# Attention, layer norm and five gated graph steps on one core: Strassen's block sums moved from accumulating DMA to VectorE

## The chip, the cores and the metric

The kernel runs on one core of a Trainium2 chip. The metric is the device time of one execution in microseconds (us). Lower is better.

A core has five engines that work side by side, each with its own queue of instructions, and waits for one another by semaphores: TensorE (PE in the profile: matrix products, its weight loads are PEld), VectorE (DVE), ScalarE (ACT), GpSimd (POOL) and SyncE (SP), which here only issues transfers (DMA). Products land in PSUM; everything else on the chip lies in SBUF.

## The reference

The input x has 16 images of 1024 rows by 128 columns, and one adjacency matrix `adj` (1024 x 1024, entries 0 or 1) serves all of them. Two layers follow each other, each with a residual and a layer norm without weights:

```python
# layer 0: graph attention
h = x @ others_weight
e = u1[:, idx1] + u2[:, idx2]            # u1 = h @ a1, u2 = h @ a2
att = softmax(where(adj > 0, leaky_relu(e), NEG_BIG), axis=1)
x = layernorm(x + att @ h + x @ self_weight)

# layer 1: five steps of a gated graph network, adj in both directions
for _ in range(5):
    m = adj @ h                           # m_in and m_out are the same here
    av = concat([m, m])
    u3 = h @ w_u3.T + b_u3
    z = sigmoid(av @ w3.T + b3 + u3)
    r = sigmoid(av @ w4.T + b4 + u3)
    hv = tanh(av @ w5.T + b5 + (r * h) @ w_u5.T + b_u5)
    h = (1 - z) * h + z * hv
out = layernorm(x + h)
```

## The kernel before

**The work of a step.** Images go in pairs q = 0 to 7 (images `one` = 2q and `two` = 2q + 1), and a pair goes through five steps s. A step has three parts. `messages(q, s, k)` makes m = adj h for both images, `gates(b, s, soon)` makes z, r, hv and the new h of one image, and `leave(b, s)` sends the new h on to the next step. The state h is kept transposed, `hT` (128 features by 1024 rows), in two halves of 128 x 512.

**High and low parts.** [...]`split` writes a block of h as two parts: ScalarE casts it to fp32r (L571), and VectorE subtracts the cast from the original for the rest (L575). A product then has two terms per chunk, and `product` (L583) issues eight matmuls for a block of 512 rows.

**Strassen.** The product of adj, as 2 x 2 quarters of 512 x 512, with the two images, whose halves form the other 2 x 2 matrix, is done in Winograd's form of Strassen's method: seven block products in place of eight. It needs sums of quarters of adj (made once, `tab`) and in each step four sums of blocks of h: s1, s2, s3 and s4. With X11, X12 the halves of `one` and X21, X22 those of `two`, the kernel overwrites in turn X22 += X21 (s1), X21 += X11, X11 += X22 (s2; X21 is s3) and X12 += X11 (s4). The signs that this needs are carried by the images themselves: even images are stored negated (`sign`). 34 of the 40 pair steps go this way; six, named in `PLAIN`, use eight plain products (`L1010`).

**How a block comes to `messages`.** `leave` turns 32 x 32 blocks of hT on VectorE (`turn`, L529), and four transfers put them in their places in a buffer X in device memory (`away`, L539); `back` (L547) loads X into a tile F. The sums are made there too: `add_to` (L559) is a transfer issued by GpSimd that adds one X to another in device memory. So a Strassen step loads seven times: x12, x11 and x22 as they are (F_x_x in the profile), and s1 to s4 after the sums (F_x_s). X buffers are [128, 512] blocks of 256 KB, and the loads and sums of one step are tied in order by the entries `("turn", "F", k)` and `("turn", "blk", k)`.

**Gates.** Each half of an image has one product u3 h into PSUM (L1099), which ScalarE copies to a second bank (gz, L1102) so that r and z can both be added to it (L1109), then tanh on ScalarE (L1112), r h on VectorE (L1119), two products for hv (L1125, L1126), tanh (L1129), and three VectorE operations to the new hT (L1136, L1143, L1150).

**Layer 0** is `layer0(b)`: the attention's products, a normalisation (`layernorm`: statistics on VectorE, the power on GpSimd, the scaling on ScalarE), and the way to the first step. `on_pe(b, what)` says where a transpose is made on TensorE instead of by VectorE and transfers: for the first two images and for the last step of the last three.

**The order.** All instructions are put down in a plan first. Each has an engine, an assumed length, a rank and the values it reads and writes; `Plan.order` then runs a small simulation. Whenever an engine is free, the ready instruction of the lowest rank is taken whose tiles are to be had. The lengths of VectorE's and ScalarE's work are taken `MARGIN` (1.2) times, and `LAG` stands for the time from one engine to another. Each engine then carries out its instructions strictly in the order that comes out. Ranks come from `rank_of` (10 per pair, 4.5 per step), `rank0` for layer 0, and small offsets `D` for each kind. So work of two or three pairs is in flight together. `IDLE` puts in transposes of the identity with the rank 9000, which are taken only where the plan sees TensorE without other work; they keep its clock up.

**Buffers.** `kinds` gives the number of tiles of each sort: `blk` 8 (split blocks), `F` 4 (loads of X, and those of layer 0 and of the output), `m` 5 (messages), `part` 1 and `yT` 2 (layer 0), `T` 3, `hT` 6, and in PSUM six banks `ps` and two `gz`.

Of the kernel before, what the change touches and what calls it, by code (L numbers as in the profile page):

```python
# [9 lines left out]
F32 = mybir.dt.float32  # L10
# [3 lines left out]
ALU = mybir.AluOpType  # L14
AX = mybir.AxisListType

P = 128
N = 1024
HALF = 512
NC = N // P  # L20
STEPS = 5
# [4 lines left out]
LOW, HIGH = -20.0, 100.0  # L26
TINY = 1e-30
PLAIN = {(0, 0), (0, 1), (0, 2), (7, 2), (7, 3), (7, 4)}
IDLE = 24


class Plan:
# [4 lines left out]

    MARGIN = 1.2  # L40
    SAME = {"PE": 0, "DVE": 60, "ACT": 60, "POOL": 60, "SP": 2500, "DMA": 0}
    LAG = {"PE": 250, "DVE": 150, "ACT": 170, "POOL": 200, "SP": 2500, "DMA": 2400}

# [87 lines left out]
def kernel(  # L131
# [51 lines left out]
    nc = tc.nc  # L183
    B = x_t.shape[0]
# [6 lines left out]
    wsi = const.tile([P, P], F32, tag="wsi", name="wsi")  # L191
# [8 lines left out]
    ident = const.tile([P, P], F32, tag="ident", name="ident")  # L200
# [10 lines left out]
    def exact(pools):  # L211

        def pool(name, bufs, space=None):
# [11 lines left out]
            "pb": (1, [P, N], F32, None),  # L225
            "blk": (8, [P, 2, NC // 2, P], F32R, None),
            "yT": (2, [P, HALF], F32, None),
            "part": (1, [P, HALF], F32, None),
            "junk": (1, [P, HALF], F32, None),
            "y0": (2, [P, NC // 2, P], F32, None),  # L230
            "hT": (6, [P, N], F32, None),
            "T": (3, [P, HALF], F32, None),
            "F": (4, [P, HALF], F32, None),
            "m": (5, [P, HALF], F32, None),
            "r": (3, [P, HALF], F32, None),
            "z": (3, [P, HALF], F32, None),
            "hv": (2, [P, HALF], F32, None),
# [21 lines left out]
        def T(t, dtype=None, shape=None):  # L259
            if t not in tiles:  # L260
                _, sh, dt, _ = kinds[t[0]]
                tiles[t] = places[t[0]].tile(
                    shape or sh, dtype or dt, tag=t[0], name="_".join(map(str, t)).replace("-", "n")
                )
            return tiles[t]
# [12 lines left out]
        plan = Plan({tag: k[0] for tag, k in kinds.items()})  # L278
# [3 lines left out]
        def pe(*a, **k):  # L282
            plan.add("PE", *a, **k)

        def dve(*a, **k):
            plan.add("DVE", *a, **k)

        def act(*a, **k):
            plan.add("ACT", *a, **k)

        def sp(*a, **k):
            plan.add("SP", *a, **k)


        D = dict(m=-0.4, pu=0.8, u=0, pr=0.0, pz=0.2, r=-0.3, pv=0.0, z=0.5, hv=0.4, h=0.6, tr=1.0, o=3.4, ln=3.5)
        D.update(out=4.2, l1=-7, l2=-6, l3=-6, l4=-4, l5=-3, l6=-2.5, l7=-1, l8=0)

        def on_pe(b, what):

            return b < 2 and what in ("y", "b") or b >= B - 3 and what == STEPS - 1  # L300

        def plain(q, s):

            return (q, s) in PLAIN

        def rank_of(b, s):
            return 10 * (b // 2) + 4.5 * s

        def rank0(b):
            return 10 * (b // 2) + -2.5  # L310

        def sign(b):

# [93 lines left out]


        def idle_():
            for j in range(4):  # L410
                nc.tensor.transpose(T(("ps", "idle"))[:, j * P : (j + 1) * P], ident, ident)


# [4 lines left out]
            pe(F, -99, lambda k=k: fill_(k), reads=[(("ident",), 0)], writes=[(("gz", "fill", k), 0)])  # L418

        for i in range(IDLE):  # L420
            pe(4 * TR, 9000, idle_, reads=[(("ident",), 0)], writes=[(("ps", "idle"), 0)])

        def self_():
            nc.vector.tensor_tensor(wsi, W("ws"), ident, ALU.add)
# [91 lines left out]
        def transposes(src, read, t, rank):  # L516


            def emit():
                for j in range(4):  # L520
                    nc.tensor.transpose(T(t)[:, j * P : (j + 1) * P], src()[:, j * P : (j + 1) * P], ident)

            pe(4 * TR, rank, emit, reads=[*read, (("ident",), 0)], writes=[(t, 0)])
# [19 lines left out]
        def back(d, t, rank, also=(), then=()):  # L543
            sp(
                450,
                rank,
                lambda: nc.sync.dma_start(T(t), T(d)[:, 0:HALF]),  # L547
                reads=[(d, 0), *also],
                writes=[(t, 0), *then],
                lag=2300,  # L550
            )

        def add_to(d, other, rank):

            plan.add(
                "POOL",
                1000,
                rank,
                lambda: nc.gpsimd.dma_start(T(d)[:, 0:HALF], T(other)[:, 0:HALF], accum_op=ALU.add),  # L559
                reads=[(other, 0), (d, 0)],  # L560
                writes=[(d, 0)],
                lag=3500,
            )

        def split(blk, src, read, rank, then=()):
# [27 lines left out]
        def layer0(b):  # L593

            first = rank0(b) - (60 if b == 0 else 0)
            rank = first + D["l1"]
# [240 lines left out]
            right = slice(HALF, N)  # L837
            for g in range(2):
                po = ("ps", "acc", b, "po", g)
                part = (yT[0], "p") if g == 0 else (("part", b), "p")  # L840

                def part_(g=g, po=po, part=part):
                    nc.vector.tensor_tensor(T(part[0]), T(po), pairs()[:, g, :], ALU.mult)

                for c0 in range(0, 4, size):
                    cs = range(c0, c0 + size)

                    def po_(g=g, po=po, cs=cs):
                        product(po, hl[0][g], quarter(g, 0), cs[0] == 0, cs[-1] == 3, cs)

                    pe(
                        2 * size * R,
                        rank,
                        po_,
                        reads=[(k, 4 * g + c, j) for k, j in ((hl[0][g], 0), (hl[0][g], 1), (("A",), 0)) for c in cs],
                        writes=[(po, 0)],
                    )
                dve(V, rank, part_, reads=[(po, 0), (pb, 0), (pb, 1)], writes=[part])

            def add_():  # L860
                nc.vector.tensor_tensor(T(yT[0]), T(yT[0]), T(("part", b)), ALU.add)

            dve(V, rank, add_, reads=[(yT[0], "p"), (("part", b), "p")], writes=[(yT[0], "s")])
            px = ("ps", "acc", b, "px")
            pe(
                F,
                rank,
                lambda: nc.tensor.matmul(T(px), wsi, T(xt)[:, left], start=True, stop=True),
                reads=[(xt, 0), (("wsi",), 0), (("part", b), "p")],
                writes=[(px, 0)],  # L870
            )
            dve(
# [13 lines left out]
            for g in range(2):  # L886
# [4 lines left out]
                    reads=[(k, 4 * g + c, j) for k, j in ((hl[1][g], 0), (hl[1][g], 1), (("A",), 1)) for c in range(4)],  # L891
                    writes=[(po2, 0)],
                )
            act(A, rank, lambda: nc.scalar.copy(T(yT[1]), T(po2)), reads=[(po2, 0)], writes=[(yT[1], 0)])

            for g in range(2):
                rank = rank0(b) + D["l5"]
# [77 lines left out]
        def messages(q, s, k):  # L975
# [5 lines left out]
            def by_chunk(t):  # L981
                return T(t).rearrange("p (c a j) -> p c a j", c=4, a=4) if s == 0 else chunks(T(t))

            def from_dram(b, g, blk, last=False):
                t = ("F", "x", *blk[1:])
                entered = [(("hT", x), "in") for x in (one, two)] if s == 0 else []
                back(
                    ("X", b, s, g), t, rank, [(("turn",), "F", k - 1), *entered], [(("turn",), "F", k)] if last else ()
                )
                split(  # L990
                    blk,
                    lambda: by_chunk(t),
                    [(t, 0), (("turn",), "blk", k - 1)],
                    rank,
                    [(("turn",), "blk", k)] if last else (),
                )

            def multiply(bank, blk, right, of, first, last, onto=()):
# [10 lines left out]

            if plain(q, s):  # L1010
                for b in (one, two):
                    blks = [("blk", b, "h", s, g) for g in range(2)]
                    if s:
                        for g in range(2):
                            from_dram(b, g, blks[g], b == two and g == 1)
                    for e in range(2):
                        bank, m = ("ps", "acc", b, s, e), ("m", b, s, e)
                        for g in range(2):
                            multiply(bank, blks[g], quarter(g, e), y(g, e), g == 0, g == 1)
                        act(  # L1020
                            A,
                            rank + D["m"],
                            lambda bank=bank, m=m: nc.scalar.copy(T(m), T(bank)),
                            reads=[(bank, 0)],
                            writes=[(m, 0)],
                        )
                return [[(("m", b, s, e), 0) for e in range(2)] for b in (one, two)]

            def X(b, g):
                return ("X", b, s, g)  # L1030

            blk = {k: ("blk", q, s, k) for k in ("x11", "x12", "x22", "s1", "s2", "s3", "s4")}
            t = [(("tab",), c, k) for c in range(4) for k in range(2)]
            from_dram(one, 1, blk["x12"])
            from_dram(one, 0, blk["x11"])
            from_dram(two, 1, blk["x22"])
            add_to(X(two, 1), X(two, 0), rank)
            from_dram(two, 1, blk["s1"])
            add_to(X(two, 0), X(one, 0), rank)
            add_to(X(one, 0), X(two, 1), rank)  # L1040
            from_dram(one, 0, blk["s2"])
            from_dram(two, 0, blk["s3"])
            add_to(X(one, 1), X(one, 0), rank)
            from_dram(one, 1, blk["s4"], True)

            a, b, c = (("ps", "acc", q, s, "a"), ("gz", q, s), ("ps", "acc", q, s, "c"))
            m = {(x, e): ("m", x, s, e) for x in (one, two) for e in range(2)}
# [107 lines left out]
        def leave(b, s):  # L1155
# [3 lines left out]
            for g in range(2):  # L1159
# [2 lines left out]
                    return T(hT)[:, g * HALF : (g + 1) * HALF]  # L1162

                k, d = ("T", b, s, g), ("X", b, s + 1, g)
                if s < STEPS - 1:
                    turn(k, h, [(hT, g)], rank + D["tr"])
                    away(k, d, rank + D["tr"])
                    continue
# [376 lines left out]
```

## Time and profile before

| | |
|---|---|
| median of 3 runs | 1603.84 us |
| lowest and highest | 1602.44 and 1603.89 us |
| span of the profiled execution | 1594.5 us |
| mean granted TensorE clock | 0.968 |
| VectorE busy | 1094.1 us |
| ScalarE busy | 891.5 us |
| L559, 136 accumulating transfers | 4.8 us to land (median) |
| L571, casts of summed blocks | 136 of 619 ns |
| L575, subtractions for them | 136 of 684 ns |
| L1136, a VectorE sum of two SBUF tiles | 684 ns |
| L411, idle transposes | 96, from 4 to 23 us |

A line of the profile's groups or waits begins with the line of the kernel and the engine, and then gives the tiles as out<-in. A wait "A <- B: t, n, longest" says that engine A stood still in front of A's instruction for t us in n cases, until B was done. A row of the table of stretches gives the length, busy time and count for PE, PEld, DVE, ACT and POOL, then the granted clock, the share of the DMA engines and the GB/s.

### The profile page before, as it was taken

Reading aid. Unit: us, or ns where it says so; the run is one execution under the profiler, and the core shown is the slowest. Engines: PE = TensorE matmul, PEld = TensorE weight load, DVE = VectorE, ACT = ScalarE, POOL = GpSimd, SP = SyncE. Lnnn points to the kernel's source line nnn. Section 1 sums busy time; section 2 is a strip of 40 time slices with the busy share of each in tenths; the row PEclk is TensorE's granted clock in tenths of the full one; section 3 lists DMA queues with packets and bytes.
Section 4 is the critical chain, followed back from the end, with each engine's and each line's share of the span. In section 5 each row is a group of like instructions: output and inputs, shape, how many; then the busy total and the mean of one; then the engine's idle time right before and its main releaser. Section 6 shows DMA issues by size and latency. Waiting matters only on the chain. (4 is left out here: it accounts for less than half of the span.)

```text
span 1594.5 us, 18201 instructions
## 1 busy us (share of the span) xinstructions
PE 1478.0 (93%) x4932; PEld 908.5 (57%) x4932; DVE 1094.1 (69%) x2625; ACT 891.5 (56%) x1792; POOL 260.1 (16%) x401
## 2 busy tenths in 40 slices
PE   8998899899998999999889989998899999999994
PEld 6665566565555556655565555665566555555552
DVE  6877678677865768668676677766678566665434
ACT  4546556565555655566555556565556555544434
POOL 0202003012120121212221121111302022101002
PEclk9999999999999999999999999999999999999997
DMA  4145666766686667776566665766667666553221
GB/s 164 60 120 158 173 157 181 185 152 161 152 225 154 145 152 169 198 166 155 142 167 189 155 158 141 185 180 157 153 154 178 169 164 139 125 127 93 78 66 42
DMA packets 245540, 238.74 MB, mean 150 GB/s; under 512 B 39007, under 2 KB 164662, under 8 KB 245430
## 3 DMA queue, kind: packets, MB, share of 16 engines
q1 hardware_dynamic: 225282, 200.99, 43.2%
q0 software_dynamic: 19584, 35.66, 15.9%
q10 hardware_dynamic: 564, 0.85, 0.2%
q8 instruction: 40, 0.66, 0.2%
q14 instruction: 70, 0.57, 0.1%
HBM read 158.07 MB, written 114.99 MB: 171 GB/s over the span
## 5 line engine op out<-in xcount | busy, mean ns | idle before, releaser
L559 POOL DMA_DIRECT2D X<-X x136 | 114.3, 840 | 891.2 <-DMA X<-X 310.5
L571 ACT CAST blk_s<-F_x_s 128x512 fp32r<-128x512 f32 x136 | 83.6, 619 | 201.9 <-DMA F_x_s<-X 198.2
L1109 PE MATMUL ps_g_r<-m,wm 128*128 128x512 f32 x320 | 162.6, 607 | 23.8 <-ACT gz L1102 22.1
L1126 PE MATMUL ps_g_v<-r,u5h 128*128 128x512 f32 x320 | 166.6, 602 | 12.5 <-DVE r L1119 12.5
L583 PE MATMUL ps_acc_a<-tab,blk_s 128*128 128x512 f32 x544 | 156.9, 430 | 17.6 <-ACT m L1052 13.3
L1125 PE MATMUL ps_g_v<-m,wm 128*128 128x512 f32 x320 | 164.3, 595 | 0.0
L1109 PE MATMUL gz<-m,wm 128*128 128x512 f32 x320 | 161.1, 604 | 0.0
L1136 DVE TENSOR_TENSOR hv<-hv,hT 128x512 f32<-128x512 f32 x160 | 109.3, 684 | 72.6 <-ACT hv L1129 72.1
L1099 PE MATMUL ps_g_r<-hT,u 128*128 128x512 f32 x320 | 154.4, 595 | 0.0
L575 DVE TENSOR_TENSOR blk_s<-F_x_s,blk_s 128x512 fp32r<-128x512 f32 x136 | 92.6, 684 | 83.8 <-ACT blk_s L571 83.5
L1119 DVE SCALAR_TENSOR_TENSOR r<-r,hT 128x512 f32<-128x512 f32 x160 | 109.3, 687 | 54.4 <-ACT r L1112 53.7
L583 PE MATMUL ps_acc_po<-adj,blk 128*128 128x512 f32 x512 | 145.5, 429 | 0.0
L583 PEld LDWEIGHTS ps_acc_a<-tab,blk_s 128*128 128x128 f32 x544 | 105.4, 198 | 62.4 <-ACT m L1052 22.3
L1112 ACT ACTIVATE r<-ps_g_r,bh 128x512 f32<-128x512 f32 x160 | 108.9, 685 | 37.3 <-PE ps_g_r L1109 37.0
L583 PEld LDWEIGHTS ps_acc_po<-adj,blk 128*128 128x128 f32 x512 | 96.1, 188 | 40.3 <-issue 17.3
L583 PE MATMUL ps_acc<-adj,blk_h 128*128 128x512 f32 x384 | 104.3, 431 | 14.2 <-ACT blk_h L571 8.6
L1112 ACT ACTIVATE z<-gz,bh 128x512 f32<-128x512 f32 x160 | 109.4, 687 | 9.6 <-PE gz L1109 9.2
L1126 PEld LDWEIGHTS ps_g_v<-r,u5h 128*128 128x128 f32 x320 | 59.9, 191 | 94.4 <-issue 57.4
L529 DVE STREAM_TRANSPOSE T<-hT 128x512 f32<-128x512 f32 x154 | 108.5, 705 | 5.7 <-DMA X<-T 3.6
L1109 PEld LDWEIGHTS ps_g_r<-m,wm 128*128 128x128 f32 x320 | 59.9, 193 | 90.7 <-issue 45.6
L1143 DVE SCALAR_TENSOR_TENSOR hv<-z,hv 128x512 f32<-128x512 f32 x160 | 108.6, 680 | 3.0 <-ACT z L1112 1.8
L1150 DVE SCALAR_TENSOR_TENSOR hT<-hv,hT 128x512 f32<-128x512 f32 x160 | 108.4, 679 | 1.8
(165 smaller groups left out, 2445.5 us busy)
## 6 DMA issues: line engine op xcount, KB each, us to landing
X<-T SPq DMA_DIRECT2D x616, 64.0 KB
X<-X POOLq DMA_DIRECT2D x136, 256.0 KB, 4.8
F_x_s<-X SPq DMA_DIRECT2D x136, 256.0 KB
F_x_x<-X SPq DMA_DIRECT2D x102, 256.0 KB
yd<-y SPq DMA_DIRECT2D x32, 256.0 KB
o<-yd SPq DMA_DIRECT2D x32, 256.0 KB
out_dram<-o SPq DMA_DIRECT2D x32, 256.0 KB
xt<-in_x_dram SPq DMA_DIRECT2D x15, 512.0 KB
```

Of the source, the lines that this page charges most:

```text
L529: nc.vector.transpose(T(t).rearrange("p (b c i) -> p b c i", b=4, c=4), turned(src()))
L559: lambda: nc.gpsimd.dma_start(T(d)[:, 0:HALF], T(other)[:, 0:HALF], accum_op=ALU.add),
L583: nc.tensor.matmul(T(bank), T(blk)[:, k, c, :], right(c), start=(first and i == 0), stop=(last and i == len(terms) - 1), skip_group_check= ...
L1099: nc.tensor.matmul(T(pr), u3, h(), start=True, stop=True)
L1109: nc.tensor.matmul(T(p_), wm[:, j, :], T(m), start=False, stop=True, skip_group_check=True)
L1112: nc.scalar.activation(T(t), T(p_), AF.Tanh, bias=bh[:, j : j + 1], scale=0.5 * sg)
L1119: lambda r=r, h=h: nc.vector.scalar_tensor_tensor(T(r), T(r), 1.0, h(), ALU.add, ALU.mult),
L1125: nc.tensor.matmul(T(pv), wm[:, 2, :], T(m), start=True, stop=False)
L1126: nc.tensor.matmul(T(pv), u5h, T(r), start=False, stop=True)
L1136: lambda hv=hv, h=h: nc.vector.tensor_tensor(T(hv), T(hv), h(), ALU.subtract),
L1143: lambda hv=hv, z=z: nc.vector.scalar_tensor_tensor(T(hv), T(z), 1.0, T(hv), ALU.add, ALU.mult),
L1150: lambda hv=hv, h=h: nc.vector.scalar_tensor_tensor(h(), T(hv), 0.5, h(), ALU.mult, ALU.add),
```

## The change

Five things change.

1. The block sums are made on VectorE. The four halves f11, f12, f21, f22 of a pair are loaded once each into tiles of a new sort G (4), in the order f11, f12, f21, f22. `halves` splits x11, x12 and x22 from them, and `add_to` becomes a VectorE addition inside those tiles. The transfers that accumulate, and three loads of each Strassen step, are gone.
2. Tiles for G come from others: F has 2 instead of 4, m has 4 instead of 5, and `part` is gone. In layer 0 the second partial product goes to yT[1] instead, and the copy into yT[1] waits for the sum that reads it.
3. The last pair is staggered: the plain steps of image 15 get a rank higher by `LATER` = 3, and step 3 of the last pair is transposed on TensorE (`TURNED`), so that its blocks are split directly from PSUM.
4. Ranks and offsets are set anew, and `MARGIN` is 1.15.
5. There are 100 idle pieces of two transposes instead of 24 of four.

```diff
-IDLE = 24
+LATER = 3
+TURNED = {(7, 3)}
+IDLE = 100
...
-    MARGIN = 1.2
+    MARGIN = 1.15
...
-            "part": (1, [P, HALF], F32, None),
...
-            "F": (4, [P, HALF], F32, None),
-            "m": (5, [P, HALF], F32, None),
+            "G": (4, [P, HALF], F32, None),
+            "F": (2, [P, HALF], F32, None),
+            "m": (4, [P, HALF], F32, None),
...
-        D = dict(m=-0.4, pu=0.8, u=0, pr=0.0, pz=0.2, r=-0.3, pv=0.0, z=0.5, hv=0.4, h=0.6, tr=1.0, o=3.4, ln=3.5)
-        D.update(out=4.2, l1=-7, l2=-6, l3=-6, l4=-4, l5=-3, l6=-2.5, l7=-1, l8=0)
+        D = dict(m=-0.4, pu=1.4, u=0.4, pr=0.8, pz=1.4, r=-0.3, pv=0.2, z=0.3, hv=0.2, h=0.6, tr=1.0, o=3.6, ln=3.9)
+        D.update(out=4.2, l1=-9, l2=-5, l3=-4, l4=-4, l5=-5, l6=-3.5, l7=-1, l8=0)
...
-            return b < 2 and what in ("y", "b") or b >= B - 3 and what == STEPS - 1
+            return b < 2 and what in ("y", "b") or b >= B - 3 and what == STEPS - 1 or (b // 2, what) in TURNED
...
-            return 10 * (b // 2) + 4.5 * s
+            return 10 * (b // 2) + 4.2 * s + (LATER if b == B - 1 and plain(b // 2, s) else 0)
...
-            return 10 * (b // 2) + -2.5
+            return 10 * (b // 2) - 1 * (1 - b % 2) + -1.0
...
-            for j in range(4):
+            for j in range(2):
                 nc.tensor.transpose(T(("ps", "idle"))[:, j * P : (j + 1) * P], ident, ident)
...
-        def add_to(d, other, rank):
-
-            plan.add(
-                "POOL",
-                1000,
-                rank,
-                lambda: nc.gpsimd.dma_start(T(d)[:, 0:HALF], T(other)[:, 0:HALF], accum_op=ALU.add),
-                reads=[(other, 0), (d, 0)],
-                writes=[(d, 0)],
-                lag=3500,
-            )
...
-                part = (yT[0], "p") if g == 0 else (("part", b), "p")
+                part = (yT[g], "p")
...
+            def from_dram(b, g, i):
+                t, x = ("G", b, s, g), ("X", b, s, g)
+                turn = [(("turn",), k, i - 1) if i else (("turn",), k - 1, 3)]
                 entered = [(("hT", x), "in") for x in (one, two)] if s == 0 else []
+                sp(0, rank, lambda: T(t), reads=[(x, 0), *turn, *entered], writes=[(t, "place"), (("turn",), k, i)], lag=0)
+                back(x, t, rank, [(t, "place")])
+                return t
...
+            def add_to(t, other):
+                dve(
+                    V,
+                    rank,
+                    lambda: nc.vector.tensor_tensor(T(t), T(t), T(other), ALU.add),
+                    reads=[(other, 0), (t, 0)],
+                    writes=[(t, 0)],
+                )
...
-            from_dram(one, 1, blk["x12"])
-            from_dram(one, 0, blk["x11"])
-            from_dram(two, 1, blk["x22"])
-            add_to(X(two, 1), X(two, 0), rank)
-            from_dram(two, 1, blk["s1"])
-            add_to(X(two, 0), X(one, 0), rank)
-            add_to(X(one, 0), X(two, 1), rank)
-            from_dram(one, 0, blk["s2"])
-            from_dram(two, 0, blk["s3"])
-            add_to(X(one, 1), X(one, 0), rank)
-            from_dram(one, 1, blk["s4"], True)
+            f11, f12, f21, f22 = (from_dram(x, g, 2 * (x == two) + g) for x in (one, two) for g in range(2))
+            halves(blk["x11"], f11)
+            halves(blk["x12"], f12)
+            halves(blk["x22"], f22)
+            add_to(f22, f21)
+            halves(blk["s1"], f22)
+            add_to(f21, f11)
+            add_to(f11, f22)
+            halves(blk["s2"], f11)
+            halves(blk["s3"], f21)
+            add_to(f12, f11)
+            halves(blk["s4"], f12, True)
...
+                if s < STEPS - 1 and on_pe(b, s):
+                    t = ("ps", "t", b, s, g)
+                    transposes(h, [(hT, g)], t, rank + D["tr"])
+                    split(
+                        ("blk", b, "h", s + 1, g),
+                        lambda t=t: T(t).rearrange("p (c a j) -> p c a j", c=4, a=4),
+                        [(t, 0)],
+                        rank_of(b, s + 1),
+                    )
+                    continue
```

More of the change, by code (lines that the diff above doesn't have):

```diff
@@ L420, in exact @@
         for i in range(IDLE):
-            pe(4 * TR, 9000, idle_, reads=[(("ident",), 0)], writes=[(("ps", "idle"), 0)])
+            pe(2 * TR, 9000, idle_, reads=[(("ident",), 0)], writes=[(("ps", "idle"), 0)])
         def self_():
@@ L860, in add_ @@
             def add_():
-                nc.vector.tensor_tensor(T(yT[0]), T(yT[0]), T(("part", b)), ALU.add)
-            dve(V, rank, add_, reads=[(yT[0], "p"), (("part", b), "p")], writes=[(yT[0], "s")])
+                nc.vector.tensor_tensor(T(yT[0]), T(yT[0]), T(yT[1]), ALU.add)
+            dve(V, rank, add_, reads=[(yT[0], "p"), (yT[1], "p")], writes=[(yT[0], "s")])
             px = ("ps", "acc", b, "px")
@@ L868, in layer0 @@
                 lambda: nc.tensor.matmul(T(px), wsi, T(xt)[:, left], start=True, stop=True),
-                reads=[(xt, 0), (("wsi",), 0), (("part", b), "p")],
+                reads=[(xt, 0), (("wsi",), 0), (yT[1], "p")],
                 writes=[(px, 0)],
@@ L893, in layer0 @@
                 )
-            act(A, rank, lambda: nc.scalar.copy(T(yT[1]), T(po2)), reads=[(po2, 0)], writes=[(yT[1], 0)])
+            act(A, rank, lambda: nc.scalar.copy(T(yT[1]), T(po2)), reads=[(po2, 0), (yT[0], "s")], writes=[(yT[1], 0)])
             for g in range(2):
@@ L982, in by_chunk, with halves @@
                 return T(t).rearrange("p (c a j) -> p c a j", c=4, a=4) if s == 0 else chunks(T(t))
-            def from_dram(b, g, blk, last=False):
-                t = ("F", "x", *blk[1:])
+            def from_dram(b, g, i):
+                t, x = ("G", b, s, g), ("X", b, s, g)
+                turn = [(("turn",), k, i - 1) if i else (("turn",), k - 1, 3)]
                 entered = [(("hT", x), "in") for x in (one, two)] if s == 0 else []
-                back(
-                    ("X", b, s, g), t, rank, [(("turn",), "F", k - 1), *entered], [(("turn",), "F", k)] if last else ()
-                )
+                sp(0, rank, lambda: T(t), reads=[(x, 0), *turn, *entered], writes=[(t, "place"), (("turn",), k, i)], lag=0)
+                back(x, t, rank, [(t, "place")])
+                return t
+            others = []
+            def halves(blk, t, last=False):
                 split(
@@ L992, in from_dram @@
                     lambda: by_chunk(t),
-                    [(t, 0), (("turn",), "blk", k - 1)],
+                    [(t, 0), (("turn",), "blk", k - 1), *(((x, 0) for x in others) if last else ())],
                     rank,
                     [(("turn",), "blk", k)] if last else (),
+                )
+                others.append(blk)
+            def add_to(t, other):
[5 more added lines that the diff above has]
+                    writes=[(t, 0)],
                 )
@@ L1011, in messages @@
                 for b in (one, two):
+                    rank = rank_of(b, s)
                     blks = [("blk", b, "h", s, g) for g in range(2)]
-                    if s:
+                    if s and not on_pe(b, s - 1):
                         for g in range(2):
-                            from_dram(b, g, blks[g], b == two and g == 1)
+                            halves(blks[g], from_dram(b, g, 2 * (b == two) + g), b == two and g == 1)
                     for e in range(2):
@@ L1027, in messages @@
                 return [[(("m", b, s, e), 0) for e in range(2)] for b in (one, two)]
-            def X(b, g):
-                return ("X", b, s, g)
             blk = {k: ("blk", q, s, k) for k in ("x11", "x12", "x22", "s1", "s2", "s3", "s4")}
             t = [(("tab",), c, k) for c in range(4) for k in range(2)]
-            from_dram(one, 1, blk["x12"])
-            from_dram(one, 0, blk["x11"])
-            from_dram(two, 1, blk["x22"])
-            add_to(X(two, 1), X(two, 0), rank)
-            from_dram(two, 1, blk["s1"])
-            add_to(X(two, 0), X(one, 0), rank)
-            add_to(X(one, 0), X(two, 1), rank)
-            from_dram(one, 0, blk["s2"])
-            from_dram(two, 0, blk["s3"])
-            add_to(X(one, 1), X(one, 0), rank)
-            from_dram(one, 1, blk["s4"], True)
+            f11, f12, f21, f22 = (from_dram(x, g, 2 * (x == two) + g) for x in (one, two) for g in range(2))
[10 more added lines that the diff above has]
+            halves(blk["s4"], f12, True)
             a, b, c = (("ps", "acc", q, s, "a"), ("gz", q, s), ("ps", "acc", q, s, "c"))
```

## The prediction

> **What bounds the kernel now.** I read the page first, then the waits of all engines, those of SyncE's DMA queue, the timeline of one long stall, and last a table of stretches.
>
> From the page: busy shares, the slices, the queues.
>
> ```profile
> PE 1478.0 (93%) x4932; PEld 908.5 (57%) x4932; DVE 1094.1 (69%) x2625; ACT 891.5 (56%) x1792; POOL 260.1 (16%) x401
> ...
> PEclk9999999999999999999999999999999999999997
> ...
> q1 hardware_dynamic: 225282, 200.99, 43.2%
> q0 software_dynamic: 19584, 35.66, 15.9%
> ```
>
> TensorE is the bound: its matmuls leave little free. A busy matmul row is not a full array, so I took the distance from one start to the next. A gate matmul starts 0.43 us after the one before (the timeline's "x2" groups, 0.86 apart), a product of the messages 0.23. The rows count 5 x 320 of the first kind and 2800 of the second (all of L583): 1600 x 0.43 + 2800 x 0.233 is 1340; self products, h products, transposes and idle transposes add some 70. So about 1410 of the 1594.5 us is work at full clock. The rest, some 180 us, is stalls, half clock and the ends. Two views name them. Columns below: total us, times, longest.
>
> ```profile
> ACT blk_s L571 <- DMA F_x_s<-X: 198.2, 87, 8.4
> ...
> DVE blk_s L575 <- ACT blk_s L571: 83.5, 52, 4.2
> ...
> PE ps_g_r L1109 <- ACT gz L1102: 22.1, 13, 5.2
> ...
> PE ps_acc_a L583 <- ACT m L1052: 13.3, 9, 3.7
> ...
> PE ps_g_v L1126 <- DVE r L1119: 12.5, 10, 3.0
> ```
>
> ```profile
> SPq L547 <- DMA X<-X: 418.6, 113, 7.9
> ```
>
> ScalarE stands 198 us in front of the cast of a summed block whose load has not landed, and VectorE stands behind it for 84. The load itself stood 419 us in SyncE's queue for the accumulating transfer that makes the sum. What TensorE then lacks is not that block but a small copy (gz at L1102, m at L1052) queued behind the cast. One case, ScalarE and then TensorE:
>
> ```profile
> 762.19 0.62 ACT L571 CAST blk_s<-F_x_s 128x512 fp32r<-128x512 f32 x1 [4.68 <-DMA F_x_s<-X]
> 762.72 1.27 ACT L816 ACTIVATE blk<-hx,rz 128x128 fp32r<-128x128 f32 x4
> ...
> 766.26 0.58 ACT L1052 COPY m<-ps_acc_a 128x512 f32<-128x512 f32 x1
> ```
>
> ```profile
> 762.14 1.02 PE L1099 MATMUL ps_g_r<-hT,u 128*128 128x512 f32 x2
> 766.90 3.56 PE L583 MATMUL ps_acc_a<-tab,blk_s 128*128 128x512 f32 x8 [3.74 <-ACT m L1052]
> ```
>
> ```profile
> 763.00:766.60 3.60, 0.16 (x1) 0.00 (x0) 1.62 (x3) 3.60 (x11) 0.00 (x0) 1.00 0.29 81
> 766.60:770.00 3.40, 3.10 (x7) 2.48 (x8) 2.98 (x11) 2.55 (x7) 0.00 (x0) 0.51 0.55 155
> ```
>
> The copy of m had its product by about 762, and ran at 766.26: a 4.68 us wait, then the work piled up behind it. TensorE stood 3.74 us, and the second stretch shows the price that follows: the clock at 0.51 for 3.4 us, so 1.7 us more.
>
> I added up all idle times over 0.2 us before matmuls in the timeline: 100 us, of them 9 before 60 us, 80 from 60 to 1480, 11 after. Of the 80, 48.7 follow within 7 us upon a ScalarE wait for F_x_s; 30.5 follow upon another wait for a transfer (F_b, o, y, x12). The mean clock of 0.968 is 51 us lost: 31 of them in 60 to 1480, in 16 spells, ten of which (17 us) come right after a stall of the F_x_s kind.
>
> The end:
>
> ```profile
> 1480.00:1574.00 94.00, 85.95 (x255) 49.36 (x253) 44.01 (x86) 42.60 (x72) 5.23 (x10) 0.95 0.21 56
> 1574.00:1595.00 21.00, 1.09 (x4) 0.72 (x4) 5.77 (x21) 5.33 (x13) 5.16 (x11) 0.54 0.26 79
> ```
>
> After 1574 TensorE has four transposes; the two last images finish together.
>
> **What the Trainium skill says.**
> - "TensorE: Matmul & The Clock Gate", Part 1: an idle window of about 3.4 us puts the array at half clock, for whole windows. The trace agrees: spells of 3.4 or 6.8 us at 0.5.
> - The same page, Part 4, says that transposes do not count as busy for that gate. The trace differs, and decides: from 12.7 to 22.9 us 72 of 98 matmuls are idle transposes, at clock 1.00; it fell at 26.0, after a stall of 2.6.
> - The same page, "Architectural detail": ScalarE and VectorE are strict FIFO. The trace agrees (766.26 above).
> - "DMA: Bandwidth & Descriptors", "SWDGE vs HWDGE vs iDMA": accumulating in a DMA is GpSimd's software path alone. The trace agrees: q0 moved 35.66 MB, which is 136 x 256 KB.
>
> **The change part by part.**
>
> Block sums. Removed: 136 accumulating transfers (median 4.8 us to land) and 102 of 238 loads for Strassen's steps (7 become 4 in 34 steps). A chain of three sums in series and a load, about 3 x 4.8 plus 2 to 3 us, becomes three VectorE adds. Price of an add: L1136, the same form (128x512 f32 in SBUF), 0.684 us; 136 x 0.684 is 93 us. By the table of stretches VectorE was busy 324 + 358 + 319 = 1001 us of the 1420 from 60 to 1480, 70%; with the adds it comes to 77%. It also loses most of its 84 us behind the casts. The casts now wait for an add of 0.7 us plus what stands ahead in VectorE's queue, not for a landing. I take three quarters of the 48.7 us of stalls (36.5) and three quarters of the 17 us of half clock (13). Transfers on the loads' path get less company (q0's 15.9% goes): 5 of the other 30.5.
>
> What it adds. ScalarE's cast waits for VectorE; behind it are again gz and m, and TensorE behind those. VectorE's longer queue reaches TensorE through r and the sums of m. Bounds: nothing, if the adds fill time in which it stood behind casts; 25 us, if its direct waits (12.5) triple. I take 8. SyncE's G loads wait for the tile's last reader, and behind them in its queue are the stores of turned halves (X<-T), from which a later step starts; they stood behind F_x_s loads for 419 us so far, so this can hardly be worse. GpSimd's row statistics stand behind no accumulate any more; ScalarE waited 31 us for them in all, of which I count nothing.
>
> Buffers. The four G tiles are one step's, and hold until the last cast. A step has about 37 us (34 from 182 to 1434). Four loads, some 5 us, then seven casts with subtractions and four adds in one line, 7 x 1.3 + 4 x 0.7, make 17. So they are hidden in TensorE's step, unless loads come late. F from 4 to 2: twelve loads per pair of images, each held some 8 us, are 96 of 380 us of slots. m from 5 to 4: the next step's first copy may wait for a gate. Neither shows in this trace; bounds 0 and 16 (all waits for m copies doubled), I take 4. `part` becoming yT[1] puts one ScalarE copy behind an add of 0.7 us: nothing, products of the gates run meanwhile.
>
> Order. Ranks and the margin (1.15) move work by a few us inside a queue; no row prices them, and I count nothing, but widen the range.
>
> Idle transposes. 200 of 0.109 us replace 96, 11 us more. They lie where the plan sees no work; the start has stalls of 9 us and two spells (3.4 and 6.8 us, 5.1 lost). I take 3 gained there, 2 lost later where the plan is wrong.
>
> The end. Image 15's last steps start later, so image 14's gates cover its loads and block casts; the step before the last is turned on TensorE (16 transposes of 0.109, 1.7 us lost). Visible loss there: stalls 10.8, half clock 5.1, and 5 in the last 18 us in which an `o` tile waits for the tile's former output. One image alone at the end fills TensorE badly and gives some back: I take 10 of 21.
>
> Sum: 36.5 + 13 + 5 + 3 + 10 - 8 - 4 - 2 - 1.7 is 51.8; 1603.84 - 51.8 gives 1552.
>
> **The rivals.**
> - Half of it is replaced: ScalarE stands for G loads or adds instead. For it: casts of x blocks, which have no sums, wait 58 us too. Against: those stalls are shorter (3.9 at most). Half the gain: 1578.
> - All goes well: all 48.7, 15 of the other stalls, 24 of clock, 14 at the end, 3 at the start, less 15: 90 us, 1514.
> - Slower: VectorE becomes the bound in a Strassen step. 77% in a strict queue with waits is near it; 2.3 us more in each of 34 steps are 78, against the 52 gained: 1630. Against: it stands 84 us behind casts now.
> - TensorE's waits only change their names: 1604.
>
> **How the numbers follow.** Likeliest (1552) 0.50, half 0.17, all well 0.15, slower 0.14, no change 0.04. So faster 0.82, same 0.04, slower 0.14. The range, 1512 to 1600, leaves out the slower case and a little below the best one; it holds the unknown of the order and both ends for VectorE's queue.
>
> **What would show it.** Right: ScalarE's wait at the casts of summed blocks falls from 198 us to under 70, and names VectorE; q0 is gone; VectorE is busy near 1180; the clock is at 0.98 or more; the stalls from 60 to 1480 fall to about 40. Wrong: waits for L1119 or L1062 above 35 us before matmuls, or loads of G that wait in SyncE's queue for a tile, as long as F_x_s did.

## The result and the profile after

The changed kernel takes 1466.28 us (median of 4 runs, 1465.17 to 1468.41) against 1603.87 of the kernel before. The ratio is 0.913, with a 95% interval of 0.910 to 0.917. It is faster by 138 us, where 52 were forecast. The direction and the first cause were right, and the size was far too small. The profiled execution of the kernel before was one of its faster ones (span 1594.5 us), so the two profiles differ by 130 us only.

The page of the changed kernel, the lines that answer to those of before:

```profile
span 1464.7 us, 17943 instructions
...
PE 1442.1 (98%) x5052; PEld 904.6 (62%) x5052; DVE 1168.4 (80%) x2757; ACT 898.9 (61%) x1792; POOL 152.9 (10%) x265
...
PEclk9999999999999999999999999999999999999998
...
q1 hardware_dynamic: 207714, 172.15, 41.1%
```

TensorE is busy 98% of a shorter span, VectorE has 74 us more to do, and the software queue of the accumulating transfers is gone. The clock's mean is 0.994. The waits of all engines (line, releaser, total us, times, longest):

```profile
ACT blk_x L561 <- DMA G<-X: 31.7, 21, 5.0
...
ACT blk_s L561 <- DVE G L998: 17.3, 17, 3.3
```

The casts of the summed blocks waited 198 us for landings; now they wait 17 us for VectorE's adds (L998). Casts of unsummed blocks waited 58 us, and wait 32. SyncE's queue, which stood 419 us for the accumulates, stands for something else now, which no wait in front of a matmul names: halves of h that are not yet turned.

```profile
SPq L541 <- DVE T L531: 300.9, 90, 14.6
```

What is left in front of matmuls, all of it:

```profile
PE ps_acc L573 <- DVE blk_h L565: 3.9, 1, 3.9
PE ps_t L523 <- DVE hT L1154: 2.8, 2, 2.4
PE gz_fill L417 <- POOL ones L383: 1.3, 1, 1.3
PE ps_g_r L1113 <- ACT gz L1106: 1.1, 2, 0.7
PE ps_p L679 <- DVE T_ws L398: 1.0, 1, 1.0
PE ps_acc_a L573 <- ACT m L1056: 0.4, 1, 0.4
```

Counted as in the prediction, the stalls fell from 100 to 11 us. Spells of half clock fell from 21 to two: 6.8 us after the 3.9 us stall, and the end. The account closes within 11 us. Stalls give 89. Half clock outside the end cost 41 us and costs 3.4, so it gives 38. The time from the last matmul to the end is 12 us where it was 17, so 5. Off go 13 us of added transposes (104 idle ones and 16 others of 0.109). That is 119, against 130 between the two profiled spans. Gaps under 0.2 us are not the rest: they sum to 0.4 us before and to nothing after. The 11 us lie inside the busy time of TensorE, which fell from 1478.0 to 1442.1 us, and what they are is not shown. So nearly all the visible loss came back, and nothing new took its place. The question is which part of the change brought it.

### The profile page after: what moved, and what is told of

Its sections match the earlier page's. It is cut to its first block, busy times and chain, and to the rows that moved or that the text cites. A ratio compares the mean times of both kernels' runs of the same rounds, so it can differ in the third digit from the quotient of the medians.

```text
span 1464.7 us, 17943 instructions
## 1 busy us (share of the span) xinstructions
PE 1442.1 (98%) x5052; PEld 904.6 (62%) x5052; DVE 1168.4 (80%) x2757; ACT 898.9 (61%) x1792; POOL 152.9 (10%) x265
## 4 chain that ended last, share of the span: by engine, by line
PE 94%; DVE 2%; DMA 1%; ACT 1%; POOL 1%; issue 0%; SPq 0%; POOLq 0%; DVEq 0%
PE ps_acc_a L573 17%; PE ps_g_r L1113 9%; PE ps_g_v L1129 9%; PE ps_g_v L1130 9%; PE gz L1113 9%; PE ps_g_r L1103 9%; PE ps_acc_c L573 8%; PE ps_acc_po L573 8%; PE ps_acc L573 6%; PE gz L573 4%; PE ps_g_ph L602 2%; PE ps_idle L413 1%; PE ps_acc_po L872 1%; PE ps_acc_px L858 1%; ACT o L510 1%; DMA blk_boot<-in_adj_dram 0%
## 5 line engine op out<-in xcount | busy, mean ns | idle before, releaser
L1130 PE MATMUL ps_g_v<-r,u5h 128*128 128x512 f32 x320 | 163.3, 592 | 0.0
L1113 PE MATMUL ps_g_r<-m,wm 128*128 128x512 f32 x320 | 158.8, 594 | 1.1 <-ACT gz L1106 1.1
L1113 PE MATMUL gz<-m,wm 128*128 128x512 f32 x320 | 157.7, 592 | 0.0
L573 PE MATMUL ps_acc_a<-tab,blk_s 128*128 128x512 f32 x544 | 146.7, 411 | 0.4 <-ACT m L1056 0.4
L573 PEld LDWEIGHTS ps_acc_a<-tab,blk_s 128*128 128x128 f32 x544 | 100.4, 188 | 34.4 <-issue 6.7
L1106 ACT COPY gz<-ps_g_r 128x512 f32<-128x512 f32 x160 | 91.5, 574 | 28.1 <-PE ps_g_r L1103 26.7
L531 DVE STREAM_TRANSPOSE T<-hT 128x512 f32<-128x512 f32 x150 | 104.9, 701 | 4.1 <-DMA X<-T 3.7
L1113 PEld LDWEIGHTS gz<-m,wm 128*128 128x128 f32 x320 | 60.5, 190 | 74.4 <-issue 74.0
L573 PE MATMUL ps_acc<-adj,blk_h 128*128 128x512 f32 x384 | 99.9, 416 | 3.9 <-DVE blk_h L565 3.9
L1133 ACT ACTIVATE hv<-ps_g_v,nb 128x512 f32<-128x512 f32 x80 | 54.9, 689 | 68.6 <-PE ps_g_v L1130 68.6
```

Of the source, the lines that this page charges most:

```text
L531: nc.vector.transpose(T(t).rearrange("p (b c i) -> p b c i", b=4, c=4), turned(src()))
L573: nc.tensor.matmul(T(bank), T(blk)[:, k, c, :], right(c), start=(first and i == 0), stop=(last and i == len(terms) - 1), skip_group_check= ...
L1106: nc.scalar.copy(T(pz), T(pr))
L1113: nc.tensor.matmul(T(p_), wm[:, j, :], T(m), start=False, stop=True, skip_group_check=True)
L1130: nc.tensor.matmul(T(pv), u5h, T(r), start=False, stop=True)
```

## The experiments

Times are medians; the ratio to the kernel before, run on the same chip beside it, has its 95% interval. Two kernels of the table whose intervals overlap are not told apart. Each kernel has its own plan, since the plan is made from its own ranks, lengths and waits. Only 'unawaited' and 'unawaited_small' have the same: their traces show the same order of instructions on every engine.

| run | us | ratio | interval |
|---|---|---|---|
| sums_alone | 1518.0 | 0.947 | 0.942 to 0.952 |
| order_alone | 1601.8 | 1.001 | 0.998 to 1.003 |
| old_order | 1500.0 | 0.936 | 0.932 to 0.941 |
| no_accumulate | 1517.6 | 0.948 | 0.943 to 0.953 |
| unawaited | 1568.6 | 0.981 | 0.978 to 0.984 |
| unawaited_small | 1522.1 | 0.949 | 0.943 to 0.955 |
| no_stagger | 1485.0 | 0.929 | 0.926 to 0.931 |
| idle_24 | 1464.2 | 0.916 | 0.913 to 0.918 |
| adds_twice | 1521.3 | 0.951 | 0.949 to 0.954 |
| offsets_old | 1488.8 | 0.929 | 0.923 to 0.934 |
| margin_old | 1483.9 | 0.926 | 0.920 to 0.931 |
| spacing_old | 1510.1 | 0.946 | 0.941 to 0.951 |
| margin_116 | 1487.5 | 0.931 | 0.926 to 0.935 |
| turned_early | 1486.1 | 0.926 | 0.920 to 0.931 |
| sums_115 | 1515.6 | 0.948 | 0.943 to 0.953 |
| before_115 | 1603.6 | 1.002 | 0.999 to 1.005 |

### Sums or order

Two theories stood against each other. Theory S: the accumulating chain starved TensorE, directly and through all that stands in the same queues. Theory O: the new order gives the slack.

**sums_alone**, from the changed kernel; the offsets D and the four transposes in an idle piece are the old ones too:

```diff
-LATER = 3
-TURNED = {(7, 3)}
-IDLE = 100
+LATER = 0
+TURNED = set()
+IDLE = 24
...
-    MARGIN = 1.15
+    MARGIN = 1.2
...
-            return 10 * (b // 2) + 4.2 * s + (LATER if b == B - 1 and plain(b // 2, s) else 0)
+            return 10 * (b // 2) + 4.5 * s
...
-            return 10 * (b // 2) - 1 * (1 - b % 2) + -1.0
+            return 10 * (b // 2) + -2.5
```

> The kernel before with the block sums on VectorE and the tiles for them (G 4, F 2, m 4, no part); ranks, margin, idle transposes and the last pair as before. Theory S (the accumulating chain starves TensorE, directly and through everything else that stands in the same queues): nearly all of the gain is here, under 1510 us, stalls before matmuls under 30 us. Theory O (the new ranks and the margin give the slack, the sums alone give what was predicted for them, about 50 us): 1540 to 1565 us, stalls 50 us or more.

1518.0: 85 us of the 138 are here. Theory S has the larger part, though not "nearly all". Stalls before matmuls fell from 100 to 51 us, not below 30.

**order_alone**, from the kernel before; with it the new D and `rank0`:

```diff
-    MARGIN = 1.2
+    MARGIN = 1.15
...
-            return 10 * (b // 2) + 4.5 * s
+            return 10 * (b // 2) + 4.2 * s
```

> The kernel before with the new offsets, ranks and margin alone; sums still by accumulating transfers. Theory S: within 20 us of before (1585 to 1625), ScalarE still waits about 200 us for summed blocks. Theory O: 1530 to 1570 us.

1601.8: no change. ScalarE still waited 227 us for summed blocks:

```profile
ACT blk_s L571 <- DMA F_x_s<-X: 226.5, 93, 10.5
```

With the accumulates in place the order is worth nothing.

**old_order**, the changed kernel with `MARGIN`, D, `rank0` and the 4.5 of before:

> The changed kernel with the old offsets, ranks and margin; sums on VectorE, idle transposes and staggered end as changed. Theory S: up to 1495 us, within 30 of the changed kernel. Theory O: 1530 us or more. If the two need each other: between these, and sums_alone and order_alone both give little.

1500.0, between the two. So the sums bring 85, idle transposes and the end together 18 (1518.0 to 1500.0), and the new order 34 (1500.0 to 1466.3), but only once the sums are on VectorE.

### What in the accumulates cost

**no_accumulate**, from the kernel before:

```diff
-            add_to(X(two, 1), X(two, 0), rank)
             from_dram(two, 1, blk["s1"])
-            add_to(X(two, 0), X(one, 0), rank)
-            add_to(X(one, 0), X(two, 1), rank)
```

and the fourth alike. The sums are left out of the computation.

> The kernel before with its four accumulating transfers per Strassen step left out; the seven loads stay, so the blocks s1 to s4 hold halves that are not summed (that part of the computation is left out). No work is added to VectorE, and the order is the old one. Theory S: the wait for the sums is what cost, so about as fast as sums_alone (within 15 us) or a little faster. Theory O: 1530 us or more. If it is the number of loads and not the sums that cost: much slower than sums_alone, 1560 us or more.

1517.6, the same as with the adds on VectorE and four loads. So three loads fewer in each step, 93 us of adds and the new tiles together change nothing under the old order. What cost was the accumulates.

**unawaited**, from the kernel before, with a scratch block S in device memory that is filled once at the start; the blocks stay unsummed:

```diff
-                lambda: nc.gpsimd.dma_start(T(d)[:, 0:HALF], T(other)[:, 0:HALF], accum_op=ALU.add),
-                reads=[(other, 0), (d, 0)],
-                writes=[(d, 0)],
+                lambda: nc.gpsimd.dma_start(T(("S", 0)), T(other)[:, 0:HALF], accum_op=ALU.add),
+                reads=[(other, 0), (d, 0), (("S", 0), 0)],
+                writes=[(("S", 0), 0)],
```

> The kernel before with its 136 accumulating transfers aimed at a scratch block in device memory: same sources, same sizes, same queue on GpSimd, one after the other, but no load waits for them (so s1 to s4 are not summed; that part of the computation is left out). If the wait for the sums starved TensorE: about 1518 us, like the kernel with no accumulates (1517.6). If it was their traffic or their place in GpSimd's queue: 1580 us or more.

1568.6, at neither value. Without any wait for the sums 51 us of the 85 are still lost. Two reasons were left: the bytes, or GpSimd's queue, in which the norms stand.

**unawaited_small**, from that kernel:

```diff
-                lambda: nc.gpsimd.dma_start(T(("S", 0)), T(other)[:, 0:HALF], accum_op=ALU.add),
+                lambda: nc.gpsimd.dma_start(T(("S", 0))[:, 0:4], T(other)[:, 0:4], accum_op=ALU.add),
```

> The run 'unawaited' with each accumulating transfer cut to 4 of 512 columns (2 KB in place of 256 KB, still 128 rows, still one after the other on GpSimd, still awaited by no load; s1 to s4 not summed). If it is the bytes in flight that delay all other landings: near the kernel with no accumulates, 1515 to 1530 us. If it is the place in GpSimd's queue (the norms' powers stand behind the accumulates): near 'unawaited', 1555 us or more.

1522.1: it is the bytes, at least in the main. GpSimd issues the same 136 instructions in the same chain, with as many packets, and TensorE hardly notices. The queue (packets, MB, share) and the issues (size, median us to landing) of 'unawaited', then those of 'unawaited_small':

```profile
q0 software_dynamic: 19584, 35.66, 16.5%
...
X<-T SPq DMA_DIRECT2D x616, 64.0 KB, 2.5
S<-X POOLq DMA_DIRECT2D x136, 256.0 KB, 4.7
...
F_x_x<-X SPq DMA_DIRECT2D x102, 256.0 KB, 3.9
```

```profile
q0 software_dynamic: 19584, 0.29, 2.3%
...
X<-T SPq DMA_DIRECT2D x616, 64.0 KB, 1.9
...
F_x_x<-X SPq DMA_DIRECT2D x102, 256.0 KB, 3.2
...
S<-X POOLq DMA_DIRECT2D x136, 2.0 KB, 3.0
```

In the median a store of a turned half lands 0.6 us later beside the full accumulates, and a load of a block 0.7 us later. Not every transfer does: the stores of the output take 2.4 us in both. The stretches, 'unawaited' first, show the DMA engines' share (last but one column, 0.69 against 0.54) and what TensorE gets done (first figure of busy time):

```profile
600.00:1000.00 400.00, 383.67 (x1280) 237.21 (x1279) 292.66 (x692) 237.22 (x476) 71.24 (x109) 0.98 0.69 169
```

```profile
600.00:1000.00 400.00, 394.88 (x1331) 245.47 (x1331) 305.66 (x743) 252.19 (x511) 76.97 (x123) 1.00 0.54 148
```

And the wait for blocks that are not summed at all, in 'unawaited' and in 'unawaited_small':

```profile
ACT blk_x L577 <- DMA F_x_x<-X: 91.1, 49, 5.0
```

```profile
ACT blk_x L577 <- DMA F_x_x<-X: 34.0, 25, 4.1
```

It reaches TensorE by the same small copies as before, in 'unawaited' and then in 'unawaited_small':

```profile
PE ps_g_r L1115 <- ACT gz L1108: 18.7, 12, 4.3
```

```profile
PE ps_g_r L1115 <- ACT gz L1108: 2.7, 2, 1.7
```

All stalls before matmuls fall from 82 to 50 us and half clock before the last matmul from 33 to 24, which is nearly all of the 44 us between the two spans.

So of the 85 us some 46 are the accumulates' bytes in the way of other transfers (1568.6 to 1522.1), some 34 the wait for the sums (1603 to 1568.6), and the rest is within the spread. Each run against the kernel before beside it gives 50 and 32. One thing is not held still: with 2 KB GpSimd's chain itself runs faster. ScalarE's waits for GpSimd's row statistics fell by 15 us (45 to 30), where its waits for landings fell by 96 (195 to 99). That speaks for the bytes, but the 46 us are not split between the two.

### The end, the idle transposes, VectorE's room

**no_stagger**, from the changed kernel:

```diff
-LATER = 3
-TURNED = {(7, 3)}
+LATER = 0
+TURNED = set()
```

> The changed kernel with LATER 0 and TURNED empty: the last pair in step, its fourth step turned by VectorE and transfers. If the end brings what was forecast for it (10 us): 1474 to 1479 us. If it brings all that was visible there (some 20 us): 1484 to 1490.

1485.0: the end is worth 19 us, all that was visible there. TensorE's order is the same in both kernels for the first 4740 matmuls, and there, at 1356 us, the two traces are 0.7 us apart. So this is the end and nothing else. The last stretches of the changed kernel and of no_stagger:

```profile
1340.00:1442.00 102.00, 102.00 (x350) 62.74 (x349) 52.12 (x112) 50.36 (x90) 11.20 (x20) 1.00 0.19 54
1442.00:1464.70 22.70, 7.48 (x22) 3.03 (x20) 10.16 (x34) 9.18 (x20) 5.11 (x12) 0.74 0.23 73
```

```profile
1340.00:1442.00 102.00, 94.61 (x302) 58.60 (x301) 47.93 (x99) 43.80 (x77) 7.05 (x16) 0.95 0.27 75
1442.00:1483.50 41.50, 19.69 (x56) 9.13 (x54) 17.60 (x52) 17.45 (x33) 8.70 (x16) 0.75 0.13 40
```

Staggered, TensorE does 350 matmuls without a stop where it did 302, with the clock whole, and 22 are left for the last stretch in place of 56.

**idle_24**, the changed kernel with `IDLE = 24` and four transposes in a piece:

> The changed kernel with 24 idle pieces of four transposes. If they bring what was forecast (1 us net): 1464 to 1470 us. If they only stand in TensorE's way: faster, about 1460. If they keep the clock up over the whole start: 1472 or more, with spells of half clock before 60 us.

1464.2, not told apart from the changed kernel. The 200 transposes did keep the clock up: with 96 there are spells of half clock at 26.5 and 47.0 us, with 200 none before 60. That bought no time.

**adds_twice**, from the changed kernel:

```diff
                     lambda: nc.vector.tensor_tensor(T(t), T(t), T(other), ALU.add),
...
+                    lambda: nc.vector.tensor_tensor(T(t), T(t), T(t), ALU.max),
```

> The changed kernel with a second VectorE operation of the same form (the maximum of the tile with itself, which leaves it as it is) behind each of the 136 adds: 93 us more on VectorE, 86% busy instead of 80. If VectorE's queue is near its limit, as the term of 8 us and the slower rival had it: 1490 us or more, with stalls at L1130 behind VectorE's r. If TensorE alone bounds the kernel and the plan hides such work: within 8 us of the changed kernel.

1521.3: 55 us dearer for 93 us of work. What stood in front of matmuls:

```profile
PE ps_acc_po L573 <- DVE blk L812: 14.3, 5, 5.6
PE ps_g_r L1120 <- ACT gz L1113: 10.7, 14, 2.5
PE ps_acc_a L573 <- ACT m L1063: 4.9, 3, 3.2
```

VectorE's own blocks (L812, the low parts of layer 0) come late, and ScalarE's small copies again. Behind what these stand is mixed: ScalarE had waited for a landing before the stall at 323 us, for GpSimd before those at 457 and 1427, for VectorE's operation on G before that at 778. In all its waits for VectorE rose from 29 to 37 us only. r, where a cost was expected, costs 1 us. Some 20 of the 55 may be the plan's (below); that the rest is VectorE's work is the likeliest reading, but is not shown apart. The first 93 us showed no cost under the old order (no_accumulate); the next do.

### The order

**offsets_old**, **margin_old** and **spacing_old**: the changed kernel with the old D alone, with `MARGIN = 1.2` alone, and with the old ranks of steps and of layer 0 alone.

> The changed kernel with the old offsets D alone; spacing of the ranks and margin as changed. The new order brings 34 us in all (1500 with all of the old order, 1466 without). If the later places of the gates' products are what gives TensorE its slack: 1490 us or more. If it is the spacing or the margin: under 1475.

> The changed kernel with the margin of 1.2 alone. If the plan's lengths matter: 1475 us or more. If the offsets carry the 34 us: 1463 to 1472.

> The changed kernel with the old ranks of steps and of layer 0 alone (4.5 per step, both images of a pair alike at -2.5). If the values act as such, the parts add up: 34 - 23 - 18 leaves nothing, so within 5 us of 1466. If the plan is one good order among worse: 1475 us or more.

1488.8, 1483.9 and 1510.1, so each alone costs 23, 18 and 44 us. All three together (old_order) cost 34. They do not add up.

**turned_early**, from idle_24, meant to take away the last stall in the middle:

```diff
-TURNED = {(7, 3)}
+TURNED = {(7, 3), (0, 1)}
```

> The changed kernel with 24 idle pieces of four, and step 1 of the first pair turned on TensorE as well: the one stall left in the middle (3.9 us before 153 us, behind a load for a plain step) and the half clock after it (6.8 us) go, for 16 transposes of 0.11 us. 1464.2 without it, so 1456 to 1460 us if that stall is TensorE's alone; 1464 or more if it only moves on.

1486.1. The stall of 4 us near 150 us is gone, and five of 1.8 to 2.4 us stand in other places, each in front of a product that waits for a small copy of ScalarE. Before four of them ScalarE had stood 3.6 to 5.0 us in front of a cast for the load of a G tile, and after four of them the clock halves for 3.4 us. An edit that helps where it was aimed lost 22 us elsewhere; the plan is another one.

**margin_116**, the smallest edit:

```diff
-    MARGIN = 1.15
+    MARGIN = 1.16
```

> The changed kernel with the margin 1.16 in place of 1.15. If the values act as such: within 4 us of the changed kernel (1462 to 1470), as 1.2 cost 18. If its plan is one good order among worse neighbours: 1475 us or more.

1487.5, 21 us slower for a step of 0.01. What stands in front of matmuls:

```profile
PE ps_g_r L1113 <- ACT gz L1106: 7.6, 9, 2.2
PE ps_acc L573 <- DVE blk_h L565: 4.3, 1, 4.3
PE ps_acc_a L573 <- ACT m L1056: 3.0, 4, 0.9
```

It is the small stalls of the old sort once more, 27 us in all in place of 11. **sums_115** (sums_alone with 1.15) and **before_115** (the kernel before with 1.15):

> The kernel with the sums alone (1518.0) with the margin at 1.15. If the smaller margin helps as such: 1495 to 1508 us. If only as part of one order: anything from 1508 to 1530.

> The kernel before with the margin at 1.15. If the accumulating transfers set its time whatever the order: within 12 us of before. If its order too is one good one among worse: 1620 us or more.

1515.6 and 1603.6: 1.15 is no better as such, and the kernel before stays where it is. So the values of the order do not act one by one. The changed kernel's plan is a good one, and five edits of its order (18 to 44 us) are all worse. Some 20 of the 34 us between the old and the new order are lost again by a step of 0.01 in one value; so that part belongs to this one plan, not to a rule about orders. No run beat the changed kernel beyond the spread.

## Why the prediction was wrong

**The bound.** Right in kind: TensorE's work, and the loss above it in stalls, half clock and ends. The 1410 us of work were too low. With 13 us of added transposes, 11 of stalls, 3 of half clock and 12 at the end they come to 1449, and the changed kernel's span is 1464.7. By its busy time (1442.1, less half clock and the added transposes) the work is nearer 1425 us, and the loss that could come back was less than the 180 named.

**The chain of causes.** Right for what it covered: ScalarE's small copies stood behind casts that stood for landings, and half clock followed. Those waits went as foretold (198 to 17 us, q0 gone, VectorE at 1168 where 1180 was named).

**The block sums, forecast at 42.5 net (36.5 + 13 + 5 - 8 - 4), measured at 85.** This is the first step that failed. "Transfers on the loads' path get less company" was put at 5 of the 30.5 us of other stalls. I gave the accumulates the cost of being waited for; unawaited and unawaited_small show that their bytes cost the more, 46 us against 34. By the profile of sums_alone the stalls fell by 48 us (99 to 51) where these terms had 29.5 net, and half clock outside the end gave 22 where 13 were named. Charges as large as the 8 and 4 were not visible either: no_accumulate, without adds and new tiles, and sums_alone, with them and three loads fewer in a step, take the same time.

**The order, counted at nothing, measured at 34.** This is the second. The range was widened for it by too little; some 20 of the 34 us hang on one plan among near neighbours, which no line of the profile before shows. order_alone shows why: with the accumulates in place the order does not matter.

**The end, forecast at 8.3 (10 less 1.7), measured at 19.** The mechanism was right and the size was off: I gave back half (10 of 21 were counted) for the last image alone, and that loss did not come.

**The idle transposes, forecast at 1.** Within the spread: idle_24 is not told apart from the changed kernel.

**The rivals.** The best case (1514) summed too little for the same reasons. The slower case, VectorE as the bound, is not what happened, but adds_twice shows that it was near.

**What stays open.** Whether better plans exist was not searched. Why this one fits, beyond that ScalarE's copies seldom stand behind a late cast (one stall of 0.7 us near 840 us follows one), is not shown. The 46 us come from two kernels with one plan. The 34 us come from kernels with plans of their own; sums_115 and before_115 moved by 2 and 3 us, so such kernels seem to move little by the plan, but that is two cases.

## What to carry to other kernels

A background transfer can have two costs: who waits for it, and whom it delays. Take the wait away and leave the bytes, then take the bytes, before you price it by its waiters alone.

When one engine's stalls all come from late neighbours, add up stalls, half clock and ends, and do not discount each: freeing the common cause can give back nearly all. And where a planner sets the order, change its input by a hair and measure: here a step of 0.01 moved the changed kernel by 21 us, and one of 0.05 the kernel before by 3, within its interval.

## What the hardware showed beyond that

- An accumulating transfer of 2 KB in 128 rows took 3.0 us to land, one of 256 KB in 128 rows 4.7, with as many packets. Most of its time was not its bytes, and yet its bytes are what the others paid for.
- Transposes of the identity held the clock at full speed: in the changed kernel they lie between 5 and 49 us, and no spell of half clock comes before 152; with half as many, two come before 60.
- Half clock did not need a long stop: in turned_early single stalls of 1.9, 2.1, 2.2 and 2.4 us were each followed by 3.4 us of it, and one of 1.75 us was not. The idle window of 3.4 us that the prediction names need not be idle throughout.
